# A planned instruction order with new lengths and ranks for a mixture-of-experts layer on one core

## The chip, the cores and the metric

The kernel runs on one core of a Trainium2 chip. The core has a matrix engine (TensorE, PE in the profile; PEld is its loading of weights), VectorE (DVE), ScalarE (ACT) and GpSimd (POOL), and SyncE (SP), which only issues DMAs here. Each engine works through its own list of instructions in a fixed order and waits at semaphores for the others. The time is the device time of one execution in microseconds (us). Three runs of the kernel before took 2497.76 to 2498.76 us, with a median of 2498.42 us.

## The reference

All values are float32. B = 16 sequences of S = 256 tokens with D = 256 channels go through 8 experts and a shared one, each with F = 1024 hidden channels; each sequence has its own weights for the experts.

```python
g = jnp.einsum('bsd,edf->ebsf', h, Wg)
u = jnp.einsum('bsd,edf->ebsf', h, Wu)
expert_outs = jnp.einsum('ebsf,efd->ebsd', jax.nn.silu(g) * u, Wd)
expert_output = jnp.einsum('be,ebsd->bsd', gating_probs, expert_outs)
shared = jnp.einsum('bsf,fd->bsd', jax.nn.silu(h @ Sg) * (h @ Su), Sd)
return x + (1.0 - sg) * expert_output + sg * shared
```

Here h is x, gating_probs is fside_Bx8_0 and sg is condB_sharedgateprob.

## The kernel before, in words

**Units.** The work is cut into 72 units: 9 experts (the shared one is the last), two halves of F (4 chunks of 128 hidden channels each), and 4 groups of 4 sequences, the group changing fastest. A unit has an up part (gate and up products, silu and their product) and a down part. In the up part the 4 chunks times 4 sequences form a grid of blocks. Blocks on its diagonal are direct products (`diagonal`): two matmuls into the bank D, an eviction by ScalarE (L673, pq), two more matmuls into the same bank, and two subtractions by VectorE that write the other half of pq. Blocks off the diagonal are made in pairs (`offdiagonal`): a shared product into a bank M with weights wp and activations xp that are sums and differences, a difference s of the pq tiles by GpSimd, a sum of M and s by VectorE that fills the bank X (`seed`), and two matmuls on top of it. So a chain goes from PE through GpSimd or VectorE back to PE for every block, and there are few PSUM banks: 3 for X, 2 for M, 1 for D, 2 for dn (the down part).

**Star units.** Units 4 to 55 use a second scheme (`unit_up`, `unit_down`). ScalarE applies silu to a gate bank (L874), and multiplies the two halves by the sequence's coefficient (L865, `scale`). VectorE multiplies the up bank by it, ScalarE copies the result (L949, h), VectorE adds it into an accumulator tile (L901, 1024 columns) and makes a sum of two blocks (low). The down part has 13 dn banks of two matmuls; ScalarE evicts each (L1103, ev), and GpSimd adds the four groups of them to sums in DRAM with DMAs that accumulate (L1117). In a star unit no VectorE instruction reads both of its inputs from SBUF.

**The other units.** Units 0 to 3 and 56 to 71 (`unit_up_w`, `unit_down_w`) multiply silu and up products with the coefficient on VectorE (L370), add and subtract tiles of h on VectorE and GpSimd, and take seven products of 512 columns for the down part. Their results go to other DRAM sums (L1041). `merge`, once for each group in these last units, adds the star units' DRAM sums to them (L1203), and `finish` adds x and writes the output.

**Weights and activations.** For each expert and half, GpSimd and ScalarE make the sums and differences of weights (wb, wp, low, side), when the group is 0. The activations' sums (xd, xp) are made once, kept in DRAM and loaded again by SP for every unit (L360).

**The order.** Nearly every instruction is recorded first, as an `Op` with an engine, a length in us, a rank and what it depends on. `Plan.run` then goes through a planned time: on each engine that is free it takes, of the operations whose inputs are there and whose buffers are free, the one of lowest rank; it holds the engine for the operation's length; and lets dependents start HOP us after its end. On PE the order by rank is kept strictly, in two lines (dn and the rest). [...] DMAs get their landing time from a length per KB. In the order of planned starts the instructions are then emitted, and each engine keeps it: the planned times decide nothing else. The lengths come from three functions of the number of columns, `dve`, `act` and `pool`; a matmul of 256 columns is planned with 0.431 us:

```python
MM = 0.431
def dve(n, stt=False):
    return (0.2 if stt else 0.12) + n * 0.00112
def act(n):
    return 0.24 + n * 0.0007
def pool(n):
    return 0.43 + n * 0.00183 if n < 4 * P else 1.365
```

RANK holds numbers that shift the ranks of the kinds of operations against each other, and the ranks at which arenas of SBUF are handed over between the two schemes ("to", "back"). Most VectorE and GpSimd instructions are recorded by a helper and have its line in the profile (L365 for two tensors, L370 with a scalar), and so have the matmuls (L646).

Of the kernel before, what the change touches and what calls it, by code (L numbers as in the profile page):

```python
# [16 lines left out]
P = 128  # L17
TB = 256
# [4 lines left out]


RANK = {
    "first": 4, "q": 2.85, "dc": 2.95, "acc": 3.05, "g": -5.35, "cp": 1.1, "seed": -0.8, "s": 0.75,
    "lagx": 1.0, "sc": 16.6, "bank": (6.6, 7.1, 8.6, 15.9, 16.4, 16.9, 17.3), "ev": 0.3, "p": 0.3, "xc":
    0.2, "st": 1.7, "qa": -2.0, "da": -1.5, "ga": -4.75, "pace": 4, "m0": 0.4, "m1": 3.25, "xm": 0, "w":
    16, "mp": 4, "m2": 1.5, "ml": 2.75, "lagw": 1.25, "wp": -0.2, "wq": 0.35, "wqa": -2.5, "wdc": 0.7,
    "ws": 1.5, "wseed": 0.2, "wxc": 1.2, "pa": -3.5, "hd": (), "ph": 7.0, "pd": 0.75, "xh": 5.25, "to":  # L30
    (-15, -6, -33, -13, -49), "back": (36, 81, -9, -33, -38, 74, 23),
}


# [29 lines left out]
class Plan:  # L64
# [8 lines left out]

    HOP = 0.25
    KB = 0.0035

    def __init__(self):
# [12 lines left out]
    def add(self, engine, length, rank, emit, deps=(), new=(), uses=(), lag=None, kb=None, port=False):  # L92
        lag = self.HOP if lag is None else lag
        op = Op(engine, length, lag, rank, emit, deps, list(new), list(uses))
        for b in [*op.new, *op.uses]:
            b.users += 1
        op.kb = kb
        op.port = port
        if engine == "PE" and op.new and op.new[0].tag == "dn" or "dn" in [b.tag for b in op.uses]:
            op.stream = 1 if engine == "PE" else None  # L100
        self.ops.append(op)
        return op
# [101 lines left out]
def kernel(  # L204
# [107 lines left out]
    TR = 0.16  # L312

    def dve(n, stt=False):
        return (0.2 if stt else 0.12) + n * 0.00112

    def act(n):
        return 0.24 + n * 0.0007

    def pool(n):  # L320
        return 0.43 + n * 0.00183 if n < 4 * P else 1.365

    ident = const.tile([P, P], F32, tag="ident", name="ident")
    make_identity(nc, ident)
# [38 lines left out]
    def tt(engine, rank, o, a, b, op, n, deps, new=(), uses=(), port=True):  # L363
        eng, length = (nc.vector, dve(n)) if engine == "DVE" else (nc.gpsimd, pool(n))
        return add(engine, length, rank, lambda: eng.tensor_tensor(o(), a(), b(), op), deps, new, uses, port=port)  # L365

    def stt(rank, o, a, c, b, op, n, deps, new=(), uses=(), port=True):
        return add(
            "DVE", dve(n, port is False), rank,
            lambda: nc.vector.scalar_tensor_tensor(o(), a(), c() if callable(c) else c, b(), ALU.mult, op),  # L370
            deps, new, uses, port=port,
        )
# [9 lines left out]
    def load_base(m, e, half, rank, ranks=None):  # L382
# [16 lines left out]
        for i, t in enumerate(POINTS):  # L399
            r, x_ = (lambda i=i: b[:, i, 1, :]), (lambda i=i: b[:, i, 0, :])  # L400
            if t == 0:
                op = v
            elif abs(t) == 1:
                op = tt("POOL", rank + 1, r, r, x_, ALU.add if t > 0 else ALU.subtract, P, [u, v], uses=[b])
            elif e == half == 0:
                op = stt(rank + 1, r, x_, float(t), r, ALU.add, P, [u, v], uses=[b])
            else:
                twice = Buf("wp", f"twice_{m}_{e}_{half}")
                op = add(
                    "ACT", act(P), rank + 1, lambda: nc.scalar.mul(twice[:, 0, :], x_(), float(t)), [u, v], [twice], [b]  # L410
                )
                op = tt("POOL", rank + 1, r, r, lambda: twice[:, 0, :], ALU.add, P, [op], [], [b, twice])
            ops.append(op)
# [225 lines left out]
    def star(n):  # L639

        return FIRST <= n < LAST

    def mm(length, rank, o, w, mv, start, stop, onto, deps, new=(), uses=()):
        return add(
            "PE", length, rank,
            lambda: nc.tensor.matmul(o(), w(), mv(), start=start, stop=stop, skip_group_check=onto),  # L646
            deps, new, uses,
        )
# [47 lines left out]
    def offdiagonal(n, unit, k, rank, pqs, pqops, consume):  # L696

        e, half, g = unit
        i, j = PAIRS[k]
        xb, xo = xp[g, k], xpop[g, k]  # L700
        mb = Buf("M", f"M_{n}_{k}")
        m1 = []
        for m in range(2):
            w, wo = pair[m, e, half, k], pairop[m, e, half, k]
            m1.append(
                mm(
                    MM, rank + m / 100, lambda m=m: mb[:, m, :], lambda w=w: w[:, 0, :], lambda: xb[:, 0, :],
                    m == 0, True, m == 1, [wo, xo[0], *m1], [mb] if m == 0 else [], [w, xb] if m == 0 else [w, xb, mb],
                )
            )  # L710
        for m in range(2):
            w, wo = pair[m, e, half, k], pairop[m, e, half, k]
            p_, q_ = pqs[m]
            s, xbank = Buf("s", f"s_{m}_{n}_{k}"), Buf("X", f"X_{m}_{n}_{k}")
            so = tt(
                "POOL", rank + m - (RANK["s"] if star(n) else RANK["ws"]), lambda s=s: s[:, :, :], lambda q_=q_: q_[:, i : j + 1 : j - i, :],
                lambda p_=p_: p_[:, 3 - j : 4 - i : j - i, :], ALU.subtract, 2 * TB, [pqops[m][i], pqops[m][j]],
                [s], [p_, q_],
            )
            seed = tt(  # L720
                "DVE", rank + m + (RANK["seed"] if star(n) else RANK["wseed"]), lambda xbank=xbank: xbank[:, :, :],
                lambda m=m: mb[:, m : m + 1, :].broadcast_to([P, 2, TB]), lambda s=s: s[:, :, :], ALU.add, 2 * TB,
                [so, *m1], [xbank], [mb, s], False,
            )
            m67 = [
                mm(
                    MM, rank + m + (LAGX if star(n) else RANK["lagw"]) + (3 + h) / 8, lambda xbank=xbank, h=h: xbank[:, h, :],
                    lambda w=w, h=h: w[:, 2 - h, :], lambda h=h: xb[:, 2 - h, :],
                    False, True, True, [seed, wo, xo[2 - h]], [], [xbank, w, xb],
                )  # L730
                for h in range(2)
            ]
            consume[m](xbank, m67, rank + m + (LAGX + RANK["xc"] if star(n) else RANK["lagw"] + RANK["wxc"]), [(j, i), (i, j)])
# [119 lines left out]
    def unit_up(n, unit):  # L853

        e, half, g = unit
        r0 = W * n
        sgs, hb = {}, {}
        acc = Buf("acc", f"acc_{n}")
# [2 lines left out]

        def scale(b, h, block, rank, deps):
            return add(
                "ACT", act(TB), rank,
                lambda: nc.scalar.mul(b[:, h, :], b[:, h, :], coef[:, e, 4 * g + block : 4 * g + block + 1]),  # L865
                [*deps, coef_op], uses=[b],
            )

        def gate(key):
            def consume(bank, deps, rank, which):  # L870
                b = Buf("sg", f"sg_{n}_{key}")
                op = add(
                    "ACT", act(2 * TB), rank,
                    lambda: nc.scalar.activation(b[:, :, :], bank[:, :, :], AF.Silu), deps, [b], [bank],  # L874
                )
                if key[0] == "d":
                    op.ahead = RANK["ga"]
                ops = [op]
                if True:
                    ops = [scale(b, h, block, rank + RANK["sc"], [op]) for h, (_, block) in enumerate(which)]  # L880
                    if key[0] == "d":
                        for o in ops:
                            o.ahead = RANK["ga"]
                sgs[key] = (b, ops)

            return consume

        def acc_pair(k, rank, x, deps, uses, port):

            i, j = PAIRS[k]  # L890

            def view():
                a = acc[:, 3 - j, :]
                return bass.AP(a.tensor, a.offset, [*a.ap[:1], [(1 + i + j) * TB, 2], [(j - i) * TB, 2], [1, TB]])

            def twice():
                a = x()
                return bass.AP(a.tensor, a.offset, [*a.ap[:1], [0, 2], [TB, 2], [1, TB]])

            op = add(  # L900
                "DVE", dve(4 * TB), rank, lambda: nc.vector.tensor_tensor(view(), view(), twice(), ALU.add),  # L901
                [*deps, *state["acc"]], [], [acc, *uses], port=port,
            )
            state["acc"] = [op]
# [60 lines left out]
        for k in range(len(PAIRS)):  # L965
            offdiagonal(n, unit, k, r0 + 2 * k, pqs, pqops, (gate(f"o{k}"), up(f"o{k}", k)))
# [376 lines left out]
    for n, unit in enumerate(units):  # L1343
        e, half, g = unit
# [140 lines left out]
```

## Time and profile before

| what | value |
|---|---|
| median of 3 runs | 2498.42 us |
| the profiled execution | 2496.74 us, span 2495.0 us |
| PE busy | 2473.5 us, 99% |
| VectorE busy | 1867.7 us, 75% |
| ScalarE busy | 1622.1 us, 65% |
| GpSimd busy | 1807.4 us, 72% |
| mean HBM traffic | 210 GB/s |
| granted clock of PE | 1.00 |

The span goes from the first to the last instruction of the profiled execution. A row of the timeline gives a start and a duration in us, the engine, the line, the operation, what is written and read, and shapes; in brackets stands the idle time of the engine before it and what ended this. A float32 matmul leaves two records, so "x2" is one matmul of 256 columns. A row of the stretches gives the stretch, then busy us and instructions of PE, PEld, VectorE, ScalarE and GpSimd, then the granted clock, the DMA engines' mean busy share, and GB/s.

### The profile page before, as it was taken

To read this page: it belongs to the slowest core of one execution; us is meant where nothing else is said; L and a number is where in the kernel's file an instruction comes from. 1 tells how busy PE (TensorE), PEld (TensorE's weight loads), DVE (VectorE), ACT (ScalarE), POOL (GpSimd) and SP (SyncE) were. 2 spreads that over 40 slices of the span, in tenths; PEclk is the share of its full clock that TensorE was granted. 3 is DMA by queue.
4 is the path that set the end of the run, shared out by engine and by line. 5 is a ranking of instruction groups with operands and counts; after the bars stand their busy time and mean duration, and the time that the engine had idled before them with its cause. 6 is when DMAs were issued, how large, how long until landed. Compare 5 with 4: busy or idle time off the path is not lost.

```text
span 2495.0 us, 34958 instructions
## 1 busy us (share of the span) xinstructions
PE 2473.5 (99%) x10886; PEld 2052.9 (82%) x10886; DVE 1867.7 (75%) x3142; ACT 1622.1 (65%) x3373; POOL 1807.4 (72%) x1947
## 2 busy tenths in 40 slices
PE   9999999999999999999999999999999999999999
PEld 5768888888888888888888888888888777777777
DVE  5787777777777777777777777777777888887787
ACT  3357777777777777787777778777777333333331
POOL 6777776768686868677776868586866788677764
PEclk9999999999999999999999999999999999999999
DMA  7546679888898888889988889888888888687776
GB/s 252 177 144 213 226 209 225 207 215 212 221 219 216 210 205 219 209 220 215 224 206 216 209 222 217 214 210 204 217 209 224 247 213 201 189 188 217 168 205 206
DMA packets 195770, 525.09 MB, mean 210 GB/s; under 512 B 16864, under 2 KB 83440, under 8 KB 186112
## 3 DMA queue, kind: packets, MB, share of 16 engines
q0 software_dynamic: 39552, 214.52, 44.6%
q1 hardware_dynamic: 154976, 307.81, 36.8%
q8 instruction: 87, 1.43, 0.2%
q14 instruction: 99, 0.81, 0.1%
q10 hardware_dynamic: 1056, 0.52, 0.1%
HBM read 290.53 MB, written 232.26 MB: 210 GB/s over the span
## 4 chain that ended last, share of the span: by engine, by line
PE 96%; DVE 2%; issue 1%; ACT 1%; DMA 0%; DVEq 0%; SPq 0%; ACTq 0%
PE dn L646 31%; PE M L646 22%; PE X L646 22%; PE D L646 19%; DVE h L365 1%; DVE X L365 0%; DVE pq L365 0%; PE dn L1291 0%; DVE big L370 0%; DVE h L370 0%; PE dn L522 0%; DMA side<-in_x_dram 0%; ACT sg L874 0%; DVE big L365 0%; ACT ev L1103 0%
## 5 line engine op out<-in xcount | busy, mean ns | idle before, releaser
L365 POOL TENSOR_TENSOR s<-pq,pq 128x512 f32<-128x512 f32 x852 | 1134.6, 1352 | 463.5 <-DVE X L365 233.8
L365 DVE TENSOR_TENSOR X<-M,s 128x512 f32<-128x512 f32 x632 | 427.1, 693 | 189.3 <-PE M L646 122.6
L646 PE MATMUL M<-xp,wp 128*128 128x256 f32 x1992 | 512.0, 379 | 1.9 <-DVE M L365 1.9
L646 PE MATMUL X<-xp,wp 128*128 128x256 f32 x1944 | 507.6, 379 | 1.5 <-DVE X L365 1.4
L646 PEld LDWEIGHTS M<-xp,wp 128*128 128x128 f32 x1992 | 378.1, 190 | 79.9 <-issue 25.6
L646 PE MATMUL D<-xd,wb 128*128 128x256 f32 x1696 | 436.9, 380 | 6.7 <-ACT sg L786 4.0
L646 PEld LDWEIGHTS X<-xp,wp 128*128 128x128 f32 x1944 | 368.8, 190 | 88.0 <-issue 34.8
L865 ACT ACTIVATE sg<-sg,coef 128x256 f32<-128x256 f32 x832 | 391.3, 509 | 1.2
L646 PEld LDWEIGHTS D<-xd,wb 128*128 128x128 f32 x1696 | 320.8, 190 | 75.0 <-issue 18.6
L1103 ACT COPY ev<-dn 128x512 f32<-128x512 f32 x456 | 267.4, 588 | 160.6 <-PE dn L646 157.2
L365 DVE TENSOR_TENSOR X<-X,sg 128x512 f32<-128x512 f32 x242 | 168.4, 696 | 172.1 <-ACT sg L865 109.1
L901 DVE TENSOR_TENSOR big<-big,X 128x1024 f32<-128x1024 f32 x242 | 292.6, 1209 | 0.0
L365 DVE TENSOR_TENSOR pq<-D,pq 128x256 f32<-128x256 f32 x568 | 229.4, 416 | 77.3 <-PE D L646 73.0
L646 PE MATMUL dn<-h,wp 128*128 128x256 f32 x1036 | 272.7, 379 | 0.3 <-ACT ev L1103 0.3
L673 ACT COPY pq<-D 128x512 f32<-128x512 f32 x284 | 166.5, 586 | 131.5 <-PE D L646 124.6
L646 PEld LDWEIGHTS dn<-h,wp 128*128 128x128 f32 x1036 | 196.6, 190 | 28.5 <-ACT ev L1103 0.7
L646 PE MATMUL dn<-h,low 128*128 128x512 f32 (+1 forms) x522 | 211.6, 507 | 0.0
L365 DVE TENSOR_TENSOR M<-M,s 128x512 f32<-128x512 f32 x220 | 152.5, 693 | 64.7 <-PE M L646 38.3
L1103 ACT COPY big<-dn 128x512 f32<-128x512 f32 x220 | 129.2, 587 | 77.5 <-PE dn L646 75.8
L874 ACT ACTIVATE sg<-X 128x512 f32<-128x512 f32 x224 | 134.1, 599 | 68.6 <-PE X L646 65.5
L1026 ACT COPY ev<-dn 128x512 f32<-128x512 f32 x122 | 71.4, 587 | 161.1 <-PE dn L646 159.5
L1117 POOL DMA_DIRECT2D star<-ev x130 | 113.6, 874 | 65.2 <-ACT ev L1103 51.4
(171 smaller groups left out, 3955.8 us busy)
## 6 DMA issues: line engine op xcount, KB each, us to landing
xp<-keep_p SPq DMA_DIRECT2D x408, 384.0 KB, 5.1
star<-ev POOLq DMA_DIRECT2D x104, 768.0 KB, 7.5
xd<-keep_d SPq DMA_DIRECT2D x136, 512.0 KB, 3.9
star<-big POOLq DMA_DIRECT2D x52, 768.0 KB, 7.6
star<-ev POOLq DMA_DIRECT2D x36, 1024.0 KB, 11.6
total<-ev POOLq DMA_DIRECT2D x17, 1024.0 KB, 8.6
star<-big POOLq DMA_DIRECT2D x16, 1024.0 KB, 11.3
total<-ev POOLq DMA_DIRECT2D x18, 768.0 KB, 7.6
```

Source lines behind the costliest of these rows:

```text
L365: return add(engine, length, rank, lambda: eng.tensor_tensor(o(), a(), b(), op), deps, new, uses, port=port)
L646: lambda: nc.tensor.matmul(o(), w(), mv(), start=start, stop=stop, skip_group_check=onto),
L673: lambda: nc.scalar.copy(p_[:, 2 - 2 * a : 4 - 2 * a, :], bank[:, :, :]), ps,
L865: lambda: nc.scalar.mul(b[:, h, :], b[:, h, :], coef[:, e, 4 * g + block : 4 * g + block + 1]),
L874: lambda: nc.scalar.activation(b[:, :, :], bank[:, :, :], AF.Silu), deps, [b], [bank],
L901: "DVE", dve(4 * TB), rank, lambda: nc.vector.tensor_tensor(view(), view(), twice(), ALU.add),
L1026: lambda ev=ev, at=at, bank=bank: nc.scalar.copy(ev[:, at, :], bank.tile.rearrange("p a t -> p (a t)")),
L1103: lambda ev=ev, at=at, bank=bank: nc.scalar.copy(ev[:, at, :], bank.tile.rearrange("p a t -> p (a t)")),
L1117: nc.gpsimd.dma_start(star_total[g][part], ev[:, 0:k, :], accum_op=ALU.add)
```

## The change

The lengths of VectorE, ScalarE and GpSimd operations become shorter, with two exceptions that are set by hand: ScalarE's scale, and GpSimd's s of the star units. HOP becomes longer. Most numbers of RANK become others. The operations, their buffers and their DMAs are the same; all engines' orders, SP's among them, come out anew. ("..." marks what is left out.)

```diff
 RANK = {
-    "first": 4, "q": 2.85, "dc": 2.95, "acc": 3.05, "g": -5.35, "cp": 1.1, "seed": -0.8, "s": 0.75,
-    "lagx": 1.0, "sc": 16.6, "bank": (6.6, 7.1, 8.6, 15.9, 16.4, 16.9, 17.3), "ev": 0.3, "p": 0.3, "xc":
-    0.2, "st": 1.7, "qa": -2.0, "da": -1.5, "ga": -4.75, "pace": 4, "m0": 0.4, "m1": 3.25, "xm": 0, "w":
-    16, "mp": 4, "m2": 1.5, "ml": 2.75, "lagw": 1.25, "wp": -0.2, "wq": 0.35, "wqa": -2.5, "wdc": 0.7,
-    "ws": 1.5, "wseed": 0.2, "wxc": 1.2, "pa": -3.5, "hd": (), "ph": 7.0, "pd": 0.75, "xh": 5.25, "to":
-    (-15, -6, -33, -13, -49), "back": (36, 81, -9, -33, -38, 74, 23),
+    "first": 4, "q": 2.35, "dc": 2.95, "acc": 2.8, "g": -5.6, "cp": 2.1, "seed": -0.05, "s": 0.75,
+    "lagx": 1.0, "sc": 16.6, "bank": (6.6, 7.1, 8.6, 15.9, 16.4, 16.9, 17.3), "ev": -0.45, "p": 1.3,
+    "xc": 0.2, "st": -1.3, "qa": -1.5, "da": -1.25, "ga": -4.5, "pace": 1, "m0": 1.4, "m1": 3.0, "xm":
+    0, "w": 16, "mp": 4, "m2": 1.0, "ml": 0.25, "lagw": 1.0, "wp": -2.45, "wq": 0.1, "wqa": -2.0, "wdc":
+    1.7, "ws": 0.75, "wseed": 0.2, "wxc": 1.45, "pa": -2.5, "hd": (), "ph": 7.25, "pd": 0.5, "xh": 5,
+    "to": (-9, -15, -12, -25, -43), "back": (12, 93, 0, -57, -32, 74, 23),
 }
...
-    HOP = 0.25
+    HOP = 0.3
...
     def dve(n, stt=False):
-        return (0.2 if stt else 0.12) + n * 0.00112
+        return (0.15 if stt else 0.09) + n * 0.00106
 
     def act(n):
-        return 0.24 + n * 0.0007
+        return 0.21 + n * 0.000625
 
     def pool(n):
-        return 0.43 + n * 0.00183 if n < 4 * P else 1.365
+        return 0.38 + n * 0.00188 if n < 4 * P else 1.28
...
                 [s], [p_, q_],
             )
+            if star(n):
+                so.length = 1.365
             seed = tt(
...
         def scale(b, h, block, rank, deps):
             return add(
-                "ACT", act(TB), rank,
+                "ACT", 0.44, rank,
```

## The prediction

> **What bounds the kernel now.** I read the page's first two parts, then the busy time by stretches of 100 us, then the timeline where the matmul engine waits.
>
> ```profile
> span 2495.0 us, 34958 instructions
> PE 2473.5 (99%) x10886; PEld 2052.9 (82%) x10886; DVE 1867.7 (75%) x3142; ACT 1622.1 (65%) x3373; POOL 1807.4 (72%) x1947
> ...
> 0.00:100.00 100.00, 94.69 (x353) 60.13 (x354) 66.14 (x127) 36.52 (x77) 70.58 (x92) 1.00 0.68 227
> 100.00:200.00 100.00, 96.59 (x369) 69.12 (x368) 82.29 (x133) 49.81 (x103) 77.82 (x85) 1.00 0.46 165
> ...
> 1200.00:1300.00 100.00, 99.69 (x462) 87.45 (x461) 72.37 (x119) 78.70 (x170) 78.68 (x93) 1.00 0.89 218
> ...
> 1900.00:2000.00 100.00, 96.42 (x406) 76.24 (x406) 86.55 (x156) 45.97 (x89) 73.07 (x74) 1.00 0.87 235
> ```
>
> PE is full, at a granted clock of 1.00 everywhere. In the timeline, matmuls of 256 columns that wait for nothing start 0.4317 us apart. I took every place where the next matmul starts later than that, and added up the excess: 4.4 us before 12 us (first loads), 8.2 us from there to 190 us, 4.6 us from 190 to 1890 us (the stage of the star units), 2.6 us from 1890 to 1942 us, 6.4 us after. That is 26.3 us of 2495, and with 1.2 us before the first matmul and 4.2 us after the last it is all that an order can touch: the change leaves the matmuls as they are, and no gain can pass some 20 us. A loss has no such limit.
>
> The star stage stalls at one spot alone, eight times, 0.58 us each:
>
> ```profile
> 341.38 0.59 ACT L1103 COPY ev<-dn 128x512 f32<-128x512 f32 x1 [0.71 <-PE dn L646]
> ...
> 341.87 0.60 ACT L874 ACTIVATE sg<-D 128x512 f32<-128x512 f32 x1
> ...
> 342.52 1.13 PE L646 MATMUL D<-xd,wb 128*128 128x256 f32 x4 [0.31 <-ACT sg L874]
> ```
>
> The single D bank comes free when ACT has read it, and ACT first evicts a dn bank whose matmul has only just ended. After 1942 us the stalls have another cause, seen here in the VectorE rows around 1973 us:
>
> ```profile
> 1973.38 4.91 DVE L365 TENSOR_TENSOR h<-h,h 128x512 f32<-128x512 f32 x1
> 1973.45 1.58 POOL L365 TENSOR_TENSOR s<-pq,pq 128x512 f32<-128x512 f32 x1
> ...
> 1982.40 0.92 PE L646 MATMUL D<-xd,wb 128*128 128x256 f32 x3 [2.17 <-ACT sg L786]
> ```
>
> An addition of 0.68 us (the same shape's usual duration) took 4.91 us while GpSimd ran, everything behind it on VectorE came late, and PE waited 2.3 us.
>
> **The change part by part: the lengths.** No instruction is added or removed, on any queue: 5512 matmuls, 3142 VectorE, 3372 ScalarE and 1679 GpSimd computations and 1054 DMAs in both built programs. Only their places move. What decides is whether the planner's new lengths can be kept by the chip.
>
> ```profile
> 1033.61 0.69 DVE L365 TENSOR_TENSOR M<-M,s 128x512 f32<-128x512 f32 x1
> 1034.21 0.69 DVE L365 TENSOR_TENSOR X<-M,s 128x512 f32<-128x512 f32 x1
> ```
>
> The row's mean duration is 693 ns, and the old length for 512 columns was 0.693 us; the new one is 0.633. But the second starts 0.60 us after the first: an engine is taken for 0.60, and 0.69 is only when the result is there. [...] The trace has the overlap at nearly every queued pair (0.60 for 512 columns, 0.33 for 256, 1.13 for 1024 against durations of 0.69, 0.41, 1.21), and so has ScalarE (0.48 against 0.59: above, the silu starts 0.49 after the eviction). So I take starts. New lengths against them: VectorE 0.633 to 0.60, 0.361 to 0.33, 1.175 to 1.13; ScalarE 0.53 to 0.48, scale 0.44 to 0.40; GpSimd 1.28 to 1.23, with the star units' s kept at 1.365. All are above what the engine is taken for. A single crossing PE, ScalarE, PE is planned at 0.3+0.53+0.3=1.13 us; the trace needs 0.25 from the last matmul's end to ScalarE's start, 0.59, and 0.05 back, 0.89. Before it was planned at 1.10. The old plan's margin per crossing (0.21) is thus kept (0.24), and waste per queued operation shrinks.
>
> **What each wait has in hand.** For each matmul that waits for another engine I went back along that engine's queue (and through one engine more) to the matmul that releases it, added starts, last duration and the 0.25 and 0.05, and set against it the matmuls that stand between, times 0.4317. Old order, the stall shown: from the dn matmul's end 0.25 + 0.48 (eviction) + 0.59 (silu) + 0.05 = 1.37, two matmuls between, 0.86: 0.51 late; the trace has 0.47 and about 0.1 for restarting. Done for all waits of the old order, it finds 4.8 of the 8.2 us from 12 to 190 us, 4.1 of 4.6 in the star stage, 2.2 of 2.6 to 1942 us, nothing after. With the restarts it is complete wherever no VectorE instruction was held up.
>
> The new order, the same way:
> - 12 to 190 us: 1.5 us is late instead of 4.8 (0.46 for a D bank at about 55 us, 1.03 near 175 us; what was late at 58, 154 and 159 us has its matmuls further off).
> - Star stage: seven lates, 3.6 us in place of 4.1. Four times near 1233, 1368, 1502 and 1637 us, D waits for its silu behind another silu and two scales: 0.25 + 0.48 + 2 x 0.40 + 0.59 + 0.05 = 2.18 against four matmuls, 1.73, is 0.45 late (0.62 where the first silu is itself late, 0.26 once). Single ones of 0.22, 0.51 and 0.74 near 1098, 1560 and 1715 us. The other units have none.
> - 1890 us on: 0.11 and 0.53 in place of 2.2.
>
> Sum 5.7 for 11.1: 5.3 us less. Seven fewer restarts at 0.07 to 0.1: 0.6 less.
>
> **The held-up VectorE instructions.** What is left of the trace's stalls, 8.6 us, stands behind VectorE instructions whose operands all lie in SBUF, as in the row of 4.91 us. There are 200 in either order, none in the star units; before, they took 93 us longer than their usual durations, and six or seven of them reached PE. [...] I counted, for each of the 200, the GpSimd work that follows in the order before one of its instructions needs VectorE. Before, 32 had 2 us or more ahead of them, and those lost 0.95 us each on average, the others 0.37. In the new order there are 15; past 1942 us, where most of the 8.6 us lie, 6 for 18. So 8.6 us becomes 8.6 x 15/32 = 4.0 if stalls follow that count, 8.6 if they don't; below it is 2 at least, and 13 if the placings are unlucky. I take 6, between the two: 2.6 less.
>
> **Queues that move.** The loads of xp have 23.1 us of matmuls from their release to their use at least in the new star stage (24.0 before; 18.8 for the tightest one at about 1941 us, 20.5 before) against 5.1 us to landing: nothing, and only a fourfold landing time would show. Stores of dn sums leave ev buffers 16.4 us or more for reuse in both, against 7.5 to 11.6. The merges' stores sit in GpSimd's queue, 80 us or more behind those that they wait for, but each issue of 0.87 to 1.2 us delays an s behind it: the same 16 in both. Waits that are instructions of their own go from 1160 to 1238 on VectorE, which is idle 25% of the time: nothing.
>
> Sum: -5.3 - 0.6 - 2.6 = -8.5 us. On the profiled execution's 2496.7 (span 2495.0 and 1.7 around it) that is 2488.2; the median of the runs is 2498.42, 1.7 more, and gives **2489.9, said as 2490**.
>
> **Rivals.** *No change (0.2):* the stalls move. For: the new order has seven lates in the star stage as the old had eight, and the held-up instructions follow an accident of neighbours; if they cost 13 us, the gain is 5.9 - 4.4 = 1.5, and the time 2497. Against: the waits from 12 to 190 us with under 0.5 us in hand fall from 13 to 6. *Slower (0.12):* a wait that repeats in each star unit, through a chain of three engines or more (M, GpSimd's s, VectorE's seed, X), where GpSimd's mean of 1.35 us is over what I added, and where new lengths have taken away the slack that absorbed it. There are 52 units: 0.16 us each eats the gain, 0.26 us makes it slower by over 0.2%, 0.5 us gives 2516. Against it: the star stage's waits on VectorE with under 0.5 us in hand are 25 for 36 before, those on ScalarE 90 for 148. Counted with whole durations for VectorE and ScalarE both, the new order is late 11.8 us in the star stage and the old one 6.0: that is the size of loss that sits in this mechanism, and the rows' starts speak against it. *Larger gain (in the range):* held-up instructions cost 2: 2486.
>
> **How the numbers follow.** 0.2% is 5 us, about what a measurement of this kernel can tell from no change. Faster 0.68, within 0.2, slower 0.12. Range 2485.5 to 2498: below by the 2 us of the last bound and half a microsecond; above by 13 us and 1 us more. It leaves out the repeating wait.
>
> **What would show it.** In the changed profile: PE between 190 and 1890 us stalls some seven times, for ScalarE's silu, under 0.8 us each; from 40 to 190 us PE idles 2 to 4 us where it idled 8.2; the 2.3 us before 1982 us is gone; VectorE's SBUF-only rows have fewer of 2 us and more. Wrong: PE idle in most star units; or SBUF-only additions of 2 to 5 us at new places with a D bank behind them.

## The result, and the profile after

The changed kernel takes 2487.06 us (median of 6 runs, 2486.94 to 2487.36), the kernel before 2498.62 us beside it (6 runs, 2497.76 to 2499.61). The ratio is 0.9954, with a 95% interval of 0.9941 to 0.9967: 8 to 15 us faster, by the medians 11.56 us. Forecast were 2490 and a range of 2485.5 to 2498. The profiled execution took 2486.94 us.

The first lines of the page, the changed kernel (busy time, share of the span, instructions of each engine):

```profile
span 2485.2 us, 35021 instructions
PE 2471.5 (99%) x10886; PEld 2054.0 (83%) x10886; DVE 1868.9 (75%) x3142; ACT 1605.0 (65%) x3373; POOL 1810.0 (73%) x1947
```

Every engine's count is the same as before; the 63 more instructions of the total (34958 before) are in none of them. The span is 9.8 us shorter. Now the stretches of the changed kernel (columns as before: busy us and instructions of PE, PEld, VectorE, ScalarE, GpSimd; clock; DMA share; GB/s):

```profile
0.00:100.00 100.00, 97.55 (x363) 62.69 (x364) 65.89 (x134) 37.43 (x79) 74.79 (x97) 1.00 0.69 231
100.00:200.00 100.00, 98.95 (x387) 72.65 (x386) 84.40 (x135) 53.88 (x114) 79.44 (x84) 1.00 0.50 179
...
1200.00:1300.00 100.00, 99.62 (x462) 87.38 (x461) 70.83 (x116) 76.46 (x167) 79.18 (x93) 1.00 0.86 213
...
1900.00:2000.00 100.00, 98.73 (x413) 77.69 (x412) 86.83 (x162) 44.07 (x84) 78.04 (x81) 1.00 0.85 227
```

In the first 200 us PE is busy for 5.2 us more than before, in the stretch from 1900 to 2000 us for 2.3 us more, and in the middle for the same 99.6 to 99.7. So the gain sits at the two ends of the star stage. As before the change, I added up wherever the next matmul starts later than its 0.4317 us, for every run of the layer, by stage (us; e1 to e5, e8 and e9 are experiments below):

| kernel | to 12 | 12 to 190 | 190 to 1890 | 1890 to 1942 | after 1942 | sum | span |
|---|---|---|---|---|---|---|---|
| before | 4.4 | 8.2 | 4.6 | 2.6 | 6.4 | 26.3 | 2495.0 |
| **after** | 4.3 | 2.3 | 4.0 | 0.2 | 6.3 | 17.1 | 2485.2 |
| e1, lengths alone | 4.4 | 2.6 | 3.5 | 2.2 | 8.9 | 21.6 | 2489.2 |
| e2, ranks alone | 4.4 | 7.8 | 1.8 | 2.0 | 4.2 | 20.2 | 2488.8 |
| e3, HOP 0.25 | 4.4 | 3.5 | 2.6 | 1.3 | 9.4 | 21.1 | 2489.8 |
| e4, HOP 0.32 | 4.3 | 1.8 | 3.2 | 0.2 | 3.8 | 13.3 | 2481.3 |
| e9, HOP 0.33 | 4.6 | 2.5 | 3.4 | 0.1 | 10.4 | 20.9 | 2488.8 |
| e8, HOP 0.34 | 4.6 | 3.0 | 2.5 | 0.1 | 4.7 | 14.9 | 2482.8 |
| e5, sums on ScalarE | 4.5 | 2.7 | 4.0 | 0.5 | 3.6 | 15.2 | 2483.0 |

Before to after, the stalls shrink by 5.9 us at the start, 0.7 in the star stage, 2.4 in the transition and 0.1 each before 12 and after 1942 us; and from the last matmul's end to the end of the span it is 3.57 us where it was 4.16. That is 9.8 us, the whole difference of the spans.

The star stage stalls at seven places. The timeline of the changed kernel at the first of the four alike:

```profile
1227.40 0.60 ACT L876 ACTIVATE sg<-M 128x512 f32<-128x512 f32 x1 [1.76 <-PE M L646]
...
1228.03 0.91 ACT L867 ACTIVATE sg<-sg,coef 128x256 f32<-128x256 f32 x2
...
1228.84 0.57 ACT L876 ACTIVATE sg<-D 128x512 f32<-128x512 f32 x1
...
1229.47 1.13 PE L646 MATMUL D<-xd,wb 128*128 128x256 f32 x4 [0.38 <-ACT sg L876]
```

This is the chain that was counted: a silu, two scales, the silu that frees D. From the matmul's end, 0.25 us ahead of 1227.40, to 1229.47 it is 2.32 us against four matmuls' 1.73: 0.59 late, and some 0.06 for the restart makes the stall of 0.65 in the trace.

After 1942 us a VectorE instruction is still held up, at a new place. Timeline of the changed kernel:

```profile
2193.95 1.19 POOL L365 TENSOR_TENSOR wp<-wp,wb 128x256 f32<-128x256 f32 x1
2194.03 4.10 DVE L365 TENSOR_TENSOR big<-big 128x512 f32<-128x512 f32 x1
2194.64 1.71 POOL L365 TENSOR_TENSOR h<-h,h 128x512 f32<-128x512 f32 x1
...
2195.86 1.71 POOL L365 TENSOR_TENSOR s<-pq,pq 128x512 f32<-128x512 f32 x1
2197.07 1.70 POOL L1205 DMA_DIRECT2D total<-big  x1
2198.06 0.41 DVE L365 TENSOR_TENSOR pq<-D,pq 128x256 f32<-128x256 f32 x1
...
2198.50 0.60 ACT L788 ACTIVATE sg<-D 128x512 f32<-128x512 f32 x1 [5.98 <-DVE pq L365]
...
2199.15 1.13 PE L646 MATMUL D<-xd,wb 128*128 128x256 f32 x4 [1.23 <-ACT sg L788]
```

An instruction usually done in 0.68 us takes 4.10 while GpSimd works; pq behind it, the silu of D and then the matmul come late, and the stall is 1.39 us (1.49 with the restart).

### The profile page after: what moved, and what is told of

Its sections match the earlier page's. It is cut to its first block, busy times and chain, and to the rows that moved or that the text cites. A ratio compares the mean times of both kernels' runs of the same rounds, so it can differ in the third digit from the quotient of the medians.

```text
span 2485.2 us, 35021 instructions
## 1 busy us (share of the span) xinstructions
PE 2471.5 (99%) x10886; PEld 2054.0 (83%) x10886; DVE 1868.9 (75%) x3142; ACT 1605.0 (65%) x3373; POOL 1810.0 (73%) x1947
## 4 chain that ended last, share of the span: by engine, by line
PE 98%; DVE 1%; ACT 1%; issue 0%; DMA 0%; SPq 0%; DVEq 0%
PE dn L646 32%; PE M L646 23%; PE X L646 22%; PE D L646 20%; DVE big L365 0%; PE dn L1293 0%; DMA side<-in_x_dram 0%; PE dn L522 0%; ACT sg L876 0%; DVE wb L365 0%; DVE ev L365 0%; DVE pq L365 0%; ACT sg L867 0%; DVE h L370 0%; DVE big L370 0%
## 5 line engine op out<-in xcount | busy, mean ns | idle before, releaser
L365 POOL TENSOR_TENSOR s<-pq,pq 128x512 f32<-128x512 f32 x852 | 1117.1, 1330 | 467.0 <-DVE X L365 338.8
L646 PE MATMUL M<-xp,wp 128*128 128x256 f32 x2052 | 526.5, 379 | 0.3 <-DVE M L365 0.3
L646 PEld LDWEIGHTS M<-xp,wp 128*128 128x128 f32 x2052 | 389.3, 190 | 89.3 <-issue 34.1
L903 DVE TENSOR_TENSOR big<-big,X 128x1024 f32<-128x1024 f32 x234 | 282.9, 1209 | 0.0
L365 DVE TENSOR_TENSOR X<-X,sg 128x512 f32<-128x512 f32 x234 | 162.9, 696 | 113.5 <-ACT sg L867 75.5
L876 ACT ACTIVATE sg<-X 128x512 f32<-128x512 f32 x234 | 140.8, 602 | 100.8 <-PE X L646 99.6
L646 PE MATMUL dn<-h,low 128*128 128x512 f32 (+1 forms) x480 | 193.1, 507 | 0.0
L365 DVE TENSOR_TENSOR low<-X,h 128x256 f32<-128x256 f32 x234 | 98.0, 419 | 103.5 <-ACT h L951 103.2
## 6 DMA issues: line engine op xcount, KB each, us to landing
star<-ev POOLq DMA_DIRECT2D x35, 1024.0 KB, 11.7
star<-big POOLq DMA_DIRECT2D x17, 1024.0 KB, 11.7
```

## Experiments

Two questions were open. Which part of the change gave the gain: lengths, ranks or HOP? And what holds VectorE up: all the work that GpSimd has ready, as the prediction's count took it, or one instruction of GpSimd? (P and Q in e7's expectation are a narrower form of the first and of the second. "Port" is the name of the planner's flag `port`, on the VectorE and GpSimd operations that it plans one after the other.) Against the reading that lengths near what an engine is taken for make a good plan stands a rival: that HOP does it, since a longer one puts more reserve behind every wait (D, where an expectation names it).

**e1: the new lengths and HOP with the ranks of before.**

```diff
 RANK = {
-    "first": 4, "q": 2.35, "dc": 2.95, "acc": 2.8, "g": -5.6, "cp": 2.1, "seed": -0.05, "s": 0.75,
...
+    "first": 4, "q": 2.85, "dc": 2.95, "acc": 3.05, "g": -5.35, "cp": 1.1, "seed": -0.8, "s": 0.75,
...
```

> New lengths and HOP with the ranks of before. Counted lates from 12 us on, as in the prediction: 1.9 us to 190 us, 2.6 in the star stage, 2.3 to 1942 us, 0.7 after; 7.5 in all, where the kernel before has 10.1 and the changed one 5.7. Theory A (the waits in hand decide, whatever number moved them): PE stalls 2 to 3 us to 190 us and 2.6 to 3 us in each of the next two; time about 2489 us, up to 3 more if more VectorE instructions are held up (26 have 2 us or more of GpSimd work ahead, 15 in the changed kernel). Theory B (the ranks did it, the lengths are neutral): about 2498.

Measured: 2490.87 us (6 runs, 2489.43 to 2491.25), ratio to the kernel before 0.9969 (0.9958 to 0.9981).

**e2: the old lengths and HOP with the new ranks.** The numbers of "back" stay those of before, since the planner finds no plan for the old lengths with the new ones.

```diff
 RANK = {
-    "first": 4, "q": 2.85, "dc": 2.95, "acc": 3.05, "g": -5.35, "cp": 1.1, "seed": -0.8, "s": 0.75,
...
+    "first": 4, "q": 2.35, "dc": 2.95, "acc": 2.8, "g": -5.6, "cp": 2.1, "seed": -0.05, "s": 0.75,
...
+    "to": (-9, -15, -12, -25, -43), "back": (36, 81, -9, -33, -38, 74, 23),
```

> New ranks (all but "back", with which the old lengths give no plan) with the lengths and HOP of before. Counted lates: 3.3 us to 190 us, 1.3 in the star stage, 1.4 to 1942 us, 1.2 after; 7.3 in all. Theory A: the start stays slow (6 to 8 us of stalls with held-up instructions), the star stage stalls 1.5 us, less than in either kernel; about 2490 to 2493 us. Theory B: as the changed kernel, 2487. Theory C (the lengths did it alone): 2498.

Measured: 2490.6 us (6 runs, 2490.51 to 2490.9), ratio 0.9969 (0.9958 to 0.9981). The stretches that tell the two apart, first e1 (the start, then the star stage):

```profile
12.00:190.00 178.00, 176.55 (x678) 122.75 (x676) 140.70 (x251) 80.45 (x169) 143.17 (x163) 1.00 0.57 200
190.00:1890.00 1700.00, 1698.99 (x7861) 1492.18 (x7860) 1243.90 (x2017) 1320.69 (x2817) 1227.26 (x1368) 1.00 0.86 215
```

and e2:

```profile
12.00:190.00 178.00, 173.29 (x654) 117.41 (x652) 137.86 (x244) 76.68 (x161) 139.08 (x160) 1.00 0.55 193
...
190.00:1890.00 1700.00, 1699.29 (x7868) 1493.96 (x7867) 1238.16 (x2020) 1324.17 (x2823) 1231.59 (x1369) 1.00 0.86 215
```

From 12 to 190 us PE gets through 678 records with the lengths alone (679 with the whole change) and 654 with the ranks alone (654 before): the start is cured by lengths and HOP. The lengths do most of it: with the new ranks and lengths at the old HOP (e3 below) the start stalls 3.5 us, with the new ranks alone 7.8, with the whole change 2.3. In the star stage the ranks alone do better (7868 records) than lengths alone (7861) and than the whole change (7858), with 1.8 us of stalls for 3.5 and 4.0. The parts don't add up: each alone is worth some 8 us, both 11.6, and the star stage is worse with both. The transition's 2.4 us come with new ranks and lengths together; since e2 kept the old "back", which hands the SBUF arenas over just there, it doesn't tell whether lengths were needed for them.

**e3, e4, e9, e8: HOP alone**, in the changed kernel.

```diff
-    HOP = 0.3
+    HOP = 0.25
```

and in the same way 0.32, 0.33 and 0.34.

> The changed kernel with HOP 0.25 in place of 0.3: every crossing is planned 0.05 us shorter, 1.03 for one over ScalarE where 0.89 is needed. Counted lates: 1.9 to 190 us, 2.0 in the star stage, 0.7 to 1942 us, 0.5 after; 5.2 in all. Theory A: 2486.5, star stage 2.2 us of stalls for 3.95; held-up VectorE instructions may add or take 3 us. Theory D (the longer HOP is what makes the new plan hold): star stage stalls more than 4 us, 2490 or more.

> The changed kernel with HOP 0.32. Counted lates: 1.0 to 190 us, 2.8 in the star stage, 0.1 to 1942 us, 0.5 after; 4.4 in all. Theory A: 2485.7, star stage 3.1 us of stalls; held-up VectorE instructions after 1942 us may add or take 3 us. Theory D: shorter than the changed kernel as well, but by no named stage.

> The changed kernel with HOP 0.33. Counted lates 1.5, 3.1, 0.0 and 0.5 us in the four stretches; 5.1 in all. Theory A: 2486.3 with the changed kernel's stalls after 1942 us, 2483.8 with those of HOP 0.32. Theory D: between HOP 0.32 (2483.1) and HOP 0.34.

> The changed kernel with HOP 0.34. Counted lates 1.5 to 190 us, 2.0 in the star stage, 0.0 to 1942 us, 0.5 after; 4.0 in all, for 5.7 in the changed kernel and 4.4 with HOP 0.32. Theory A: 2485.2 with the changed kernel's held-up instructions after 1942 us (6.3 us of stalls there), 2482.7 with those of HOP 0.32 (3.8 us); the star stage stalls 2.2 us. Theory D (the longer HOP as such gives the gain): less than the 2483.1 of HOP 0.32.

| HOP | 0.25 (e3) | 0.30 (after) | 0.32 (e4) | 0.33 (e9) | 0.34 (e8) |
|---|---|---|---|---|---|
| median, us | 2487.7 | 2487.06 | **2483.14** | 2490.52 | 2484.56 |
| runs, us | 2487.33 to 2491.6 | 2486.94 to 2487.36 | 2483.11 to 2483.28 | 2489.04 to 2490.76 | 2484.4 to 2488.62 |
| ratio to before | 0.9962 | 0.9954 | 0.994 | 0.9965 | 0.9947 |
| 95% interval | 0.995 to 0.9975 | 0.9941 to 0.9967 | 0.9927 to 0.9954 | 0.9952 to 0.9979 | 0.9935 to 0.996 |

There is no trend in HOP. All stalls but those after 1942 us sum to 11.7, 10.8, 9.5, 10.5 and 10.2 us, those after it to 9.4, 6.3, 3.8, 10.4 and 4.7, and the medians go up and down with the latter. (The trace of HOP 0.25 is of its longest execution, 3.9 us over its median: that is in its 9.4 us.) The kernel before took 2498.38 us beside e3 and e4, and 2498.53 beside e8 and e9, so the columns can be compared. HOP deals new neighbours to the SBUF-only VectorE instructions; which of them PE waits for decides; this is read from the traces, and no run moves one such neighbour alone. That a longer HOP helps as such is refuted: 0.33 is 7.4 us slower than 0.32. The version with 0.32 is the best of the study and beats both kernels, by a lucky draw as much as by a rule.

**e5: fewer SBUF-only instructions on VectorE.** Same plan, but VectorE's additions and subtractions of h tiles in the units outside the star stage are emitted as ScalarE copies of one operand. The additions are left out of the computation; it is where their operands lie that is in question.

```diff
             def sum_(engine, r, out_, x_, y_, op, deps, new):
-                return tt(
+                o = tt(
...
                 )
+                if engine == "DVE":
+                    o.emit = lambda: nc.scalar.copy(out_[:, :, :], x_[:, :, :])
+                return o
```

> The changed kernel, same plan, but the additions that VectorE makes of two h tiles in the units outside the star stage are copies of one of them on ScalarE (the addition is left out, and the output is another). Some 120 of the 200 SBUF-only VectorE instructions are gone. Theory A (these are held up by GpSimd and stall PE): stalls after 1942 us fall from 6.3 us to 2 or less, time about 2482 us. Rival (PE stalls there for another reason, such as ScalarE's or GpSimd's own queue): stalls stay at 5 to 7 us, time 2486 to 2488, or more as ScalarE gets 0.48 us per copy.

Measured: 2484.77 us (5 runs, 2484.64 to 2484.89), ratio to before 0.9941 (0.9927 to 0.9954), 2.3 us below the changed kernel by the medians and 2.2 by the spans. VectorE has 3028 instructions for 3142. The timeline of e5 at the place shown for the changed kernel:

```profile
2193.56 0.61 ACT L991 COPY big<-big 128x512 f32<-128x512 f32 x1
2193.73 1.03 PE L646 MATMUL X<-xp,wp 128*128 128x256 f32 x4
2193.99 0.70 DVE L365 TENSOR_TENSOR M<-M,s 128x512 f32<-128x512 f32 x1 [0.96 <-POOL wp L365]
...
2197.17 1.03 PE L646 MATMUL D<-xd,wb 128*128 128x256 f32 x4
```

The instruction of 4.10 us is a copy of 0.61 us on ScalarE, VectorE goes on, and D's matmul has no wait in brackets. The stalls near 1987, 2197 and 2204 us (1.10, 1.39 and 0.29, with 0.10 of restart on top of the first two) are gone, and after 1942 us 3.6 us are left of 6.3. What is left stands at 1957 us (0.66, a counted wait) and behind SBUF-only instructions of `merge` and `finish` that this edit kept (0.83 at 2187, 1.53 at 2465 us). So these instructions are what PE waited for, as the prediction said. That it is their operands, and not only that VectorE has 114 fewer, e5 doesn't tell; e6 shows it below (1.73 us with both operands in SBUF, 0.69 with one in PSUM). The saving is half of what I expected, since I hadn't seen that two of the stalls belong to `merge` and `finish`.

**e6: VectorE's addition beside GpSimd's, by themselves.** A small kernel, without the reference's computation. GpSimd does k additions of 512 columns between SBUF tiles, and VectorE one addition `held`, which starts just behind the first of them:

```python
r = [new() for _ in range(k)]
add(nc.gpsimd, d[:, 0:8], mark, mark)
for i in range(k):
    add(nc.gpsimd, r[i], a, w[i])
add(nc.vector, held, d, second)
```

GpSimd's addition of 8 columns lets VectorE go; `second` is an SBUF tile, or a PSUM bank.

> The port alone; of the layer nothing is computed. An addition of two SBUF tiles of 512 columns on VectorE is let go just ahead of k GpSimd additions of 512 columns that wait for nothing, k = 1, 2, 4, 8; then k = 4 with one input in PSUM; then k = 4 where each GpSimd addition waits for an instruction of ScalarE that is long done; three times over. Lock for one instruction: VectorE's addition takes 0.7 to 2 us for every k. Port kept while GpSimd has work ready: 0.7 plus about 1.23 k, some 2, 3.2, 5.6 and 10.5 us. With the input in PSUM 0.7 us. With satisfied waits: as without them if only readiness counts; about 2 us if a wait makes GpSimd give the port up.

The timeline of e6: k = 1; k = 8 with GpSimd's row; k = 4 with one operand in PSUM.

```profile
3.43 1.74 DVE L52 TENSOR_TENSOR t<-t,c 128x512 f32<-128x512 f32 x1 [0.32 <-POOL t L52]
...
14.87 10.25 POOL L52 TENSOR_TENSOR t<-a,c 128x512 f32<-128x512 f32 x8
14.94 1.73 DVE L52 TENSOR_TENSOR t<-t,c 128x512 f32<-128x512 f32 x1 [0.31 <-POOL t L52]
...
25.63 0.69 DVE L52 TENSOR_TENSOR t<-t,bank 128x512 f32<-128x512 f32 x1 [0.31 <-POOL t L52]
```

With two SBUF operands it takes 1.73 to 1.74 us for k = 1, 2, 4 and 8 alike, 1.05 over its 0.68: it waits for the GpSimd instruction that runs, and not for the seven behind it. With an operand in PSUM it takes 0.69. GpSimd's additions with ScalarE waits in front of them, long fulfilled, give 1.73 again.

**e7: the same, with VectorE coming later.** VectorE first has up to three additions that write PSUM and read one operand from it, so that it comes to `held` at another moment of GpSimd's row (five of 512 columns; also two, and eight of 128).

```diff
-        add(nc.vector, held, d, second)
+        first = True
+        for m in ahead:
+            add(nc.vector, hold[:, 0:m], bank[:, 0:m], d[:, 0:m] if first else c[:, 0:m])
+            first = False
+        add(nc.vector, held, d, c)
```

> The port alone again; of the layer nothing is computed. Five GpSimd additions of 512 columns back to back, and ahead of VectorE's addition of two SBUF tiles stand VectorE instructions with one input in PSUM (none; 64, 256, 512 columns; 512 twice; 512 twice and 256), so that it comes up 0 to 1.5 us after the run began. Then a run of two behind 512, and a run of eight with 128 columns behind 256. In the kernel the long waits stand right behind another VectorE instruction, in the middle of a GpSimd instruction. Theory P (once GpSimd's next instruction has been let in, the whole run goes first): 1.7 us with nothing ahead, as measured; 4 us and more where it comes up after the middle of the first GpSimd instruction; the run of two ends it at 1.7 to 2.5. Theory Q (the lock passes over at the end of the running instruction always; the long waits come from DMA issues of GpSimd): 0.7 to 2 us everywhere.

The timeline of e7, two additions of 512 columns ahead:

```profile
31.47 6.59 POOL L52 TENSOR_TENSOR t<-a,c 128x512 f32<-128x512 f32 x5
31.55 0.70 DVE L52 TENSOR_TENSOR hold<-bank,t 128x512 f32<-128x512 f32 x1 [0.31 <-POOL t L52]
32.28 0.70 DVE L52 TENSOR_TENSOR hold<-bank,c 128x512 f32<-128x512 f32 x1
32.89 1.61 DVE L52 TENSOR_TENSOR t<-t,c 128x512 f32<-128x512 f32 x1
```

It took 1.55 and 1.73 us with none ahead, 1.59 with 64 columns, 1.39 with 256, 1.13 with 512, 1.61 with two of 512, 1.15 with a third of 256; 1.13 before a row of two and 1.00 before eight of 128 columns. That is never more than the rest of one GpSimd instruction. That VectorE is held up for as long as GpSimd has work ready, on which the prediction's count rests, is refuted for additions that wait for nothing.

## Why the prediction was right, and where not

**PE full, and only stalls to win: right.** The nine kernels differ by their stalls and little else: span less stalls is 2468.7 before, 2468.1 after, and 2467.6 to 2468.7 in the experiments.

**Lengths: right, by the starts in the trace.** In the trace before, the second of two queued additions starts 0.60 us after the first, whose row is 0.69 long. Counted with whole durations of VectorE and ScalarE the star stage is 11.8 us late where it was 6.0; by the starts, 3.6 us where it was 4.1. The trace after has 3.95, restarts included, with 4.63 before. By its lengths the plan can be kept: e1, which is lengths and HOP alone, takes away 5.6 of the 5.9 us that the start gave.

**What each wait has in hand: right, place by place.** Star stage, forecast against measured: 0.22 and 0.25 (at 1094 us), 0.62 and 0.65, 0.62 and 0.65, 0.26 and 0.32, 0.51 and 0.63, 0.62 and 0.65, 0.74 and 0.80. At the start 0.46 and 0.51, 1.03 and 1.20; in the transition and after it 0.11 and 0.14, 0.53 and 0.66. There are no lates of this kind that weren't counted, apart from one of 0.28 us at 126 us. The rest of each is the restart. This count took only durations, starts and the two hops of the old trace, and the order of the new program.

**Held-up VectorE instructions: the step that failed.** I took a gain of 2.6 us from it, most of it after 1942 us, where the count of instructions with 2 us or more of GpSimd work ahead fell from 18 to 6. The sum came out near, by luck (stalls beyond the counted lates, with restarts: 10.8 us before, 7.1 after, 3.7 less for 3.2 with 0.6 of restarts), and the place did not: after 1942 us they shrank from 6.4 to 6.3, with 0.66 a counted wait, and the gain was made at the start. The 200 instructions took 88.2 us over their usual durations for 92.9 before, those with 2 us and more over it fell from 8 to 6, and new ones had a D bank behind them: what I had named as a sign of being wrong did come, at 1988 and 2199 us, in exchange for the stall at 1982 us. The 2.6 us come from a count of all the work that GpSimd has ready, and no run shows that such work holds VectorE up: in e6 `held` takes 1.73 to 1.74 us with one GpSimd instruction and with eight, and in e7 1.73 at most. Work behind the running instruction costs nothing there: most of what was counted was no risk.

In e6 and e7 VectorE's addition waits for one instruction of GpSimd, 1.05 us at most. In the kernels that isn't all: the 4.10 us at 2194 us go past three of GpSimd's additions and into a DMA issue, and the 4.91 us of before past seven rows. A wait for one instruction alone doesn't give them. What goes with them is a DMA issue of GpSimd. In the nine traces of the layer, 840 SBUF-only VectorE instructions lost over 0.2 us. 223 of these had a DMA issue running somewhere from 3 us ahead of their start to 0.7 us behind it, and 54 of the 223 lost over 2 us; of the other 617, 2 did. The issue may be over by then (the instruction of 3.51 us at 119 us starts 0.5 us after one). After 1942 us the instructions with such an issue near them were 41 before and are 43 now, which fits stalls that stayed as they were. GpSimd's rows are also longer there, three in a row of 1.70 or 1.71 us at starts 1.21 apart, where in e6 only the one next to `held` is that long (1.71) and the others take 1.26. No experiment put a DMA issue into GpSimd's row by itself, so that it is the cause, and how, stays **open**.

**The rivals.** No change (stalls only move) is what happened after 1942 us, and there alone. A wait that repeats in each star unit did not come: seven units of 52 stall, as counted. A larger gain by held-up instructions at 2 us is what e4 shows is possible.

**The sum.** Forecast 8.5 us; measured 11.56 between medians. On the same terms the stalls gave 9.1. The rest is 0.1 us before 12 us, 0.6 after the last matmul, for which the prediction had nothing, and 1.8 us that lie in the profiled executions: before, it ran 1.9 us under the median of the six runs, and after, 0.1. The prediction had carried the 1.7 us between profile and median over to the new kernel; that term was wrong. The last section shows what most likely makes it: a halved clock for 3.4 us, which by the mean clock (under 1.000 in 24 of 29 executions) the kernel before meets in most of them, and the changed one in none of its six.

## What to carry to other kernels

Where a planner's order feeds one full engine, count each wait's reserve in the new program with starts (0.60 us here), not durations (0.69), from the old trace: the result was good to 0.2 us at each place. Set lengths just above what an engine is taken for; and give no value to a change of order for what depends on chance neighbours, such as an SBUF-only VectorE instruction beside GpSimd: there five values of one constant spread 7 us, so draw several orders and measure them. Taking SBUF-only instructions off VectorE looks a surer remedy than placing them well: e5 points to it, though it leaves the additions out.

## What the hardware showed unexpected

A stall of PE can cost more than itself: three of 2.45 to 3.14 us cost 1.64 to 1.67 us on top. The stretches around the longest one, in e9 (HOP 0.33; PEclk is the third number from the end):

```profile
2190.00:2197.00 7.00, 7.00 (x28) 5.02 (x28) 6.96 (x9) 2.27 (x5) 7.00 (x7) 1.00 0.85 175
2197.00:2200.50 3.50, 0.76 (x4) 0.33 (x2) 3.50 (x2) 1.17 (x2) 3.50 (x4) 1.00 1.04 174
2200.50:2204.00 3.50, 3.27 (x8) 2.62 (x9) 2.67 (x5) 0.00 (x0) 1.43 (x2) 0.51 0.90 89
2204.00:2210.00 6.00, 6.00 (x24) 4.15 (x23) 3.93 (x9) 1.18 (x2) 3.73 (x5) 1.00 0.67 208
```

and the instructions there, from its timeline:

```profile
2194.74 5.32 DVE L365 TENSOR_TENSOR big<-h,big 128x512 f32<-128x512 f32 x1
...
2200.73 2.07 PE L646 MATMUL M<-xp,wp 128*128 128x256 f32 x4 [2.97 <-DVE X L365]
```

A VectorE instruction held up for 5.32 us makes PE wait 3.14 us; then the granted clock is 0.5 for 3.413 us, two matmuls take 2.07 us instead of 1.03, and 1.67 us more are lost. The same follows a stall of 2.58 us in e3 (1.64 us lost) and one of 2.45 us at the end of e1 (1.67). Stalls of 2.33 and 2.12 us before had no such drop.

The stall's length alone does not decide. From the first change of the clock in a trace to each later one it is a whole multiple of 3.413 us, in all nine traces (730 times before, 726 after). Counted by such stretches, called windows here, PE stood idle for 2.25 (e1), 2.33 (e3) and 2.94 us (e9) of the window after which the clock fell, and for 2.02 us at most where it didn't; that was in the trace before, whose stall near 1980 us began 0.4 us ahead of its window.

So by this count a stall of some 2.3 us falls on one side or the other by where the windows lie. The first change of the clock stands 4.2 us into the span before and 6.5 us after; that it also differs between executions of one kernel no trace shows, but the times on record look like it. In the 29 executions of the kernel before that ran beside the experiments, the mean granted clock is 1.000 in 5, 0.999 in 13 and 0.998 in 11, and the medians of the three groups are 2496.66, 2498.38 and 2500.19 us: steps of 1.7 and 1.8 us, where one drop costs 1.64 to 1.67 and takes by estimate 0.0007 off the mean clock (half of 3.413 us in 2497). In e1 the two executions at 1.000 took 2489.43 and 2489.53 us, the four at 0.999 took 2490.80 to 2491.25. The changed kernel's six all have 1.000; its longest stall is 1.6 us. So some 1.7 us of its gain is most likely this drop avoided. It remains an inference: of the kernel before only an execution without a drop was traced. In e3 a drop explains 1.64 of the 3.9 us between the traced execution and the median. A stall of the length of those three is to be priced with 1.64 to 1.67 us on top, and one of some 2.3 us perhaps, which the prediction's list of stalls did not have.
